# A scan kernel's last image: part of its norm beside its scans, one PSUM state less in half of the two-state steps, fp8 weights cast once

## The chip, the cores and the metric

The kernel runs on one core of a Trainium2 chip. The metric is device time in microseconds; three runs of the kernel before gave 11327.04, 11332.17 and 11333.0, median 11332.17. The profile is one further execution of 11308.41. Engines: PE (TensorE), DVE (VectorE), ACT (ScalarE), POOL (GpSimd), SP (SyncE, which issues the DMAs); PEld is PE's weight load.

## The reference, cut to what matters

Input is four images of 64 x 64 x 96. Layer 0 adds a selective-scan block with 192 channels to a group norm of x. Layer 1 does the same in the frequency domain: a 2-D real FFT, a block with 384 channels on 64 x 33 points, the inverse FFT. Layers 2 and 3 are token layers: linear attention, then a feed-forward net whose weights and activations are rounded to fp8 (e5m2). The block, shortened:

```python
xs = cross_scan(silu(conv(x_in)))          # 4 directions k: rows, columns, both reversed
dt, B, C = split(xs @ x_proj); delta = softplus(dt @ dt_w + dt_b)
h = h * exp(delta * A) + (delta * u) * B   # 16 states n per channel, serial in l
y = sum_n h * C (+ D * u)
y = layernorm(merge(y, 4 directions)) * silu(z)
out = y @ out_proj
q = lambda x: float_quantize(x, 5, 2)      # feed-forward: q(x), q(W), q(b)
```

## The kernel before, in words

**Scans.** Work is channels on partitions (three chunks c of 128), positions on the free axis, cut into segments of 512 (layer 0) or 512, 512, 384, 384, 320 (layer 1). There are six phases: two for layer 0 (two images each, 4 directions x 8 segments) and four for layer 1 (one image each, 4 x 5 segments). Directions run in the order 0, 2, 1, 3; 2 and 3 are reversed, 1 and 3 are those in which layer 1's rows lie in natural order. A segment has 12 steps: 4 quarters q of the states times 3 chunks c. A step has four states j, one DVE scan each (L710):

- ACT makes exp(delta A) (L682), in SBUF for j = 0, 1 and in PSUM for j = 2, 3. Inputs of j = 0, 1 are made by ACT (L646) and brought to PSUM by PE transposes (L678); those of j = 2, 3 by POOL (front_b, L700).
- State 0 of each step stays in PSUM and DVE multiplies it by C (multiply_kept, L728); in every other step state 3 too. The names in Step.kept, (0, 3) or (0,), say which. The other two or three states go to SBUF, and POOL multiplies them in one instruction (multiply, L747) after a small copy of the last column (L744); for kept states ACT copies that column (keep_state, L735).
- PE adds all products into acc by transposing matmuls (L757); close_chunk writes y to DRAM, one tile for directions 0 and 2, one for 1 and 3.

**Order.** Engines run in program order; scans() writes it out by hand. DMAs are all issued by SP, with eight in flight before one waits for an earlier one. All other work is a queue of tasks (Env), generators that yield between stages; each step has three slots, and rate / 3 says how many stages a slot gets. A stage that yields LATE runs in the slot at a step's end only. Each phase queues its tasks when its first segment begins: end1(b), the norm, out_proj, inverse FFT and tokens of image b, runs beside the scans of image b + 1. What is left when the scans end is run at once.

**Tail.** The last image's end1 runs after all scans, in a form with several workers (Env.wide > 1): gated (merge of directions L432, L438, mean L452, L456, variance L463, scaling L470, product with the gate L477 or L481) in three workers over the row blocks of 8, 8, 6, 6 and 5 rows, with out_proj (L1019) and the att write (L1028); then inverse (L1106, L1117) and tokens. tokens loads sixteen weight tiles per image (L1183) and casts w1, w2, b1, b2 of both layers to fp8 on DVE (L1189), b1 and b2 back to fp32 (L1191).

Of the kernel before, what the change touches and what calls it, by code (L numbers as in the profile page):

```python
# [7 lines left out]
F32 = mybir.dt.float32  # L8
F16 = mybir.dt.float16
F8 = mybir.dt.float8e5  # L10
# [8 lines left out]
NB, HH, WW, CH = 4, 64, 64, 96  # L19
# [4 lines left out]
SM = 512  # L24
LATE, BURST = "late", "burst"

RATES = [1.6, 2.35, 2.85, 2.85, 2.85, 2.85]
EXP_LN = "natural_log_exp_and_others"


# [127 lines left out]
class Block:  # L158
# [226 lines left out]
                    nc.sync.dma_start(out=gz[:, c, p0 * 64 : p1 * 64], in_=zh[:, : pr * 64])  # L385
                    yield

    def gated(self, E, g, io, out_proj):

# [6 lines left out]
        with E.pool(f"{cfg.pre}nm{g}") as sp:  # L396
            wo = sp.tile([P, C, self.w["wo"].shape[2]], F32, name=f"{cfg.pre}_wo_{g}", tag="wo")
            nc.sync.dma_start(out=wo, in_=self.w["wo"])

            def load(b, i, r, n):  # L400
# [10 lines left out]

            def worker(w):

                blocks = list(enumerate(cfg.rows))[w::W]
                todo = iter([(b, i, r + i, min(2, n - i)) for b, (r, n) in blocks for i in range(0, n, 2)])
                nxt = load(*next(todo))
                for _ in range(9 if W == 1 else 3):
                    yield
# [71 lines left out]
class Phase:  # L490

    def __init__(self, blk, g, io, needs, side, rate):
        self.blk, self.g, self.io, self.needs, self.side, self.rate = blk, g, io, needs, side, rate


class Seg:


    def __init__(self, ph, k, a, S, first, last):
        self.ph, self.blk, self.cfg = ph, ph.blk, ph.blk.cfg
        self.k, self.a, self.S, self.first, self.last = k, a, S, first, last
        self.rev = k >= 2
        self.nm = f"{self.cfg.pre}_{ph.g}_{k}_{a}"
        self.blocks = [(t, min(P, S - t)) for t in range(0, S, P)]
        full = S // P

        self.runs = [(0, full, P)] + ([(full, full + 1, S % P)] if S % P else [])
        self.bx, self.b, self.c, self.acc, self.u, self.after = {}, {}, {}, {}, None, None  # L510


class Step:


    def __init__(self, z, q, c):
        self.z, self.q, self.c = z, q, c
        self.nm = f"{z.nm}_{q}_{c}"
        self.kept = (0, 3) if (C * q + c) % 2 else (0,)
        self.hk = {}  # L520
        self.px, self.ay = {}, {}


def scans(tc, ctx, phases, ident):
# [14 lines left out]

    segs = []  # L540
    for ph in phases:
        for k in (0, 2, 1, 3):
            order = ph.blk.cfg.segs[::-1] if k >= 2 else ph.blk.cfg.segs
            segs += [Seg(ph, k, a, S, i == 0, i == len(order) - 1) for i, (a, S) in enumerate(order)]

    for z, after in zip(segs, segs[1:]):
        z.after = after
# [251 lines left out]
    with tc.manual_schedule(engines=IN_ORDER):  # L799
# [43 lines left out]
        for i, st in enumerate(steps):  # L843
            z, q, c, S = st.z, st.q, st.c, st.z.S
            nxt = steps[i + 1] if i + 1 < len(steps) else None
            if q == 0 and c == 0:
                after = z.after
                fresh = at == 0 or z.ph is not segs[at - 1].ph
                if fresh:
                    z.ph.io["y"] = [z.blk.dram_tile(f"y{j}", (2, z.cfg.L, C * P), z.ph.g) for j in range(2)]  # L850
                open_segment(z, segs[at - 1] if at else None)
                if after:
                    E.require(after.ph.needs[after.k % 2])
                pgen, pwants = prepare(after) if after else none, None
                at += 1
            if fresh and q == 0 and c == C - 1:
                for fn, arg in z.ph.side:
                    E.add((fn, arg), fn(E, arg))
            if c == 0:
                if q + 1 < NQ:  # L860
                    fetch_b(z, q + 1)
                elif after:
                    drain(pgen)
                    more = Pieces(after, 0, 4)
                    fetch_b(after, 0)
            if c == 1:
                if q + 1 < NQ:
                    fetch_c(z, q + 1)
                elif after:
                    fetch_c(after, 0)  # L870
            if older:
                add_rest(older)
            if before and 3 in before.kept:
                keep_state(before, 3)
                add_kept(before, 3)
            scan(st, 0)
            front_y(st, 2)
            if nxt:
                front_x(nxt)
            multiply_kept(st, 0)  # L880
            keep_state(st, 0)
            add_kept(st, 0)
            front_y(st, 3)
            long = burst()
            if before:
                multiply(before)
            if nxt:
                front_b(nxt)
            scan(st, 1)
            if nxt:  # L890
# [262 lines left out]
NT = LTOK // P  # L1153


def tokens(E, ins, consts, ident, x1, b, out):

# [5 lines left out]
    with E.pool(f"tk{b}") as sp:  # L1163
# [10 lines left out]
        def weights(ly):  # L1174

            nm, w, bufs = f"{b}_{ly}", {}, min(W, 2)
            for name, shape in (
                ("wqkv", [A, 3 * CH]), ("wqt", [CH, A]), ("wff", [CH, CH]), ("bff", [A, CH]),
                ("w1", [CH, 4 * CH]), ("w2", [P, 3, CH]), ("b1", [P, 3]), ("b2", [P, CH]),
            ):  # L1180
                t = w[name] = sp.tile(shape, F32, name=f"{name}_{nm}", tag=name, bufs=bufs)
                src = ins[f"l{ly}_{name}"]
                nc.sync.dma_start(out=t, in_=src.to_broadcast([P, CH]) if name == "b2" else src)  # L1183
            yield w
            for name in ("w1", "w2", "b1", "b2"):
                t = w[name]
                r = sp.tile(list(t.shape), F8, name=f"q{name}_{nm}", tag=f"q{name}", bufs=bufs)
                yield LATE
                nc.vector.tensor_copy(r, t, saturate=False)  # L1189
                if name in ("b1", "b2"):  # L1190
                    nc.vector.tensor_copy(t, r)  # L1191
                else:
                    w[name] = r

        loads = [weights(ly) for ly in (2, 3)]
        ws = [next(loads[0])] + ([next(loads[1])] if W > 1 else [])
# [3 lines left out]
        yield  # L1200
        yield
        for load in loads[: len(ws)]:
            yield from load

        def norm_all(nm):

# [155 lines left out]
        for ly in (2, 3):  # L1362
            nm = f"{b}_{ly}"
            if len(ws) < ly - 1:
                ws.append(next(loads[1]))
                yield from loads[1]
            q = ws[ly - 2]
            wq = q["wqkv"]
            if W == 1:
# [34 lines left out]
def build(tc, ins, consts, out):  # L1404
    nc = tc.nc
    with ExitStack() as ctx:
# [31 lines left out]
        x1 = [dram.tile([LTOK, CH], F32, name=f"x1_{b}", tag=f"x1_{b}") for b in range(NB)]  # L1438
        single = [dict() for _ in range(NB)]

        def flip0(E, g):
            yield from blk[0].flip(E, g, pairs[g])

# [11 lines left out]
        def begin1(E, b):  # L1455
# [2 lines left out]
            yield from blk[1].project(E, b, io)  # L1458
            yield from blk[1].gate(E, b, io)

        def end1(E, b):
            io = single[b]
            att = dram.tile([HH, WF, 2 * CH], F32, name=f"att_{b}", tag="att", bufs=NB)
            put = out1(att, b)
            yield from blk[1].gated(
                E, b, io, lambda E, *a: put(E, blk[1], *a)
            )
            yield
            rest = tokens(E, ins, consts, ident, x1[b], b, out)
# [15 lines left out]
        needs = [[None, (flip0, 0)], [(begin0, 1)] * 2]  # L1485
        with ExitStack() as inner:
            phases = [Phase(blk[0], g, pairs[g], needs[g], sides[g], RATES[g]) for g in range(2)] + [
                Phase(blk[1], b, single[b], [(begin1, b)] * 2, sides[2 + b], RATES[2 + b]) for b in range(NB)
            ]
            scans(tc, inner, phases, ident)  # L1490
        with ExitStack() as tail:
            alone(tail, end1, 3).finish()
# [113 lines left out]
```

## Time and profile before

| | us |
|---|---|
| median of the runs | 11332.17 |
| profiled execution | 11308.41 |
| its span, first to last instruction | 11306.6 |
| busy DVE / POOL / ACT / PE | 9899.2 / 9405.2 / 9384.7 / 9021.5 |
| layer 0, two phases | 217 to 2668, 2668 to 5112 |
| layer 1, four phases | 5112, 6582, 8007, 9476 to 10912 |
| tail: norm and out_proj / weights and inverse / tokens | to 11063 / to 11136 / to 11306.6 |

The mean granted clock of PE is 0.90. A line of groups reads: line, engine, operation, output <- inputs, shapes, count, busy time, mean ns of one, idle time of the engine before them and what ended it. In a table by stage each row is a window in us with the busy time (and count) of PE, PEld, DVE, ACT and POOL, the granted clock, the DMA engines' busy share, and GB/s. In the chain of waits each piece is start, length, and what ran or was waited for.

### The profile page before, as it was taken

To read this page: it belongs to the slowest core of one execution; us is meant where nothing else is said; L and a number is where in the kernel's file an instruction comes from. 1 tells how busy PE (TensorE), PEld (TensorE's weight loads), DVE (VectorE), ACT (ScalarE), POOL (GpSimd) and SP (SyncE) were. 2 spreads that over 40 slices of the span, in tenths; PEclk is the share of its full clock that TensorE was granted. 3 is DMA by queue.
4 is the path that set the end of the run, shared out by engine and by line. 5 is a ranking of instruction groups with operands and counts; after the bars stand their busy time and mean duration, and the time that the engine had idled before them with its cause. 6 is when DMAs were issued, how large, how long until landed. Compare 5 with 4: busy or idle time off the path is not lost. (4 is left out here: it accounts for less than half of the span.)

```text
span 11306.6 us, 163986 instructions
## 1 busy us (share of the span) xinstructions
PE 9021.5 (80%) x54944; PEld 6600.5 (58%) x54944; DVE 9899.2 (88%) x10695; ACT 9384.7 (83%) x19648; POOL 9405.2 (83%) x7464
## 2 busy tenths in 40 slices
PE   5678788777888888888899888887788777887775
PEld 2555555556666656656676665665566555665554
DVE  6889999889999998999888798989989889889864
ACT  3779999999888998998778788878888788878853
POOL 2999999989988998998788798878888779888750
PEclk9889999889999999999889899998899888998887
DMA  5655555556666556555543545442244223542242
GB/s 146 144 130 130 133 129 123 155 156 153 156 161 140 129 144 140 134 142 169 156 134 119 136 136 157 150 113 94 92 145 138 93 90 107 158 120 94 82 130 38
DMA packets 1208406, 1468.97 MB, mean 130 GB/s; under 512 B 482759, under 2 KB 1020559, under 8 KB 1149063
## 3 DMA queue, kind: packets, MB, share of 16 engines
q1 hardware_dynamic: 1207559, 1458.48, 47.8%
q8 instruction: 434, 7.11, 0.3%
q14 instruction: 413, 3.38, 0.1%
HBM read 1221.74 MB, written 236.50 MB: 129 GB/s over the span
## 5 line engine op out<-in xcount | busy, mean ns | idle before, releaser
L747 POOL TENSOR_TENSOR h_l<-h_l,bc_l 128x1536 f32<-128x1536 f32 (+2 forms) x1728 | 4567.8, 2643 | 184.0 <-DVE h_l L710 68.1
L700 POOL TENSOR_TENSOR h_l<-du_l,bc_l 128x512 f32<-128x512 f32 (+2 forms) x3456 | 3966.7, 1170 | 770.1 <-PE acc_l L757 718.1
L646 ACT ACTIVATE bx_l<-dut_l,bt_l 128x192 f32<-128x192 f32 (+2 forms) x6272 | 2756.4, 499 | 0.3
L757 PEld LDWEIGHTS acc_l<-ident,h_l 128*128 128x128 f32 (+1 forms) x15840 | 2047.7, 155 | 689.2 <-issue 325.9
L757 PE MATMUL acc_l<-ident,h_l 128*128 128x128 f32 (+1 forms) x15840 | 2326.3, 299 | 135.9 <-POOL h_l L747 135.6
L682 ACT ACTIVATE ax_l<-delta_l,l_alog 128x512 f32<-128x512 f32 (+2 forms) x3456 | 2140.4, 667 | 0.0
L710 DVE TENSOR_TENSOR_SCAN h_l<-b_l,state_l,h_l 128x512 f32<-128x512 f32 (+2 forms) x1263 | 1389.1, 1121 | 114.2 <-ACT b_l L682 106.6
L678 PE MATMUL b_l<-ident,bx_l 128*128 128x128 f32 (+1 forms) x6817 | 1200.5, 295 | 227.1 <-DVE h_l L710 220.2
L678 PEld LDWEIGHTS b_l<-ident,bx_l 128*128 128x128 f32 (+1 forms) x6817 | 842.9, 149 | 829.5 <-DVE h_l L710 476.8
L682 ACT ACTIVATE b_l<-delta_l,l_alog 128x512 f32<-128x512 f32 (+2 forms) x1948 | 1221.0, 627 | 107.7 <-DVE k_l L728 32.0
L710 DVE TENSOR_TENSOR_SCAN b_l<-ax_l,state_l,b_l 128x512 f32<-128x512 f32 (+2 forms) x842 | 956.5, 1136 | 194.1 <-PE b_l L678 191.3
L757 PE MATMUL acc_l<-ident,k_l 128*128 128x128 f32 (+1 forms) x5117 | 836.9, 294 | 334.3 <-DVE k_l L728 320.1
L678 PE MATMUL ab_l<-ident,bx_l 128*128 128x128 f32 x5312 | 900.9, 298 | 246.5 <-DVE h_l L710 237.7
L682 ACT ACTIVATE ab_l<-delta_l,l_alog 128x512 f32<-128x512 f32 x1326 | 913.8, 689 | 149.0 <-DVE h_l L710 70.0
L678 PEld LDWEIGHTS ab_l<-ident,bx_l 128*128 128x128 f32 x5312 | 648.5, 151 | 622.2 <-DVE h_l L710 452.4
L710 DVE TENSOR_TENSOR_SCAN h_l<-ax_l,state_l,b_l 128x512 f32<-128x512 f32 (+2 forms) x841 | 951.2, 1131 | 42.1 <-PE b_l L678 40.4
L710 DVE TENSOR_TENSOR_SCAN h_l<-ab_l,state_l,h_l 128x512 f32<-128x512 f32 x743 | 920.2, 1261 | 73.2 <-ACT ab_l L682 46.7
L728 DVE TENSOR_TENSOR k_l<-b_l,bc_l 128x512 f32<-128x512 f32 (+2 forms) x1460 | 895.4, 613 | 50.2
L757 PE MATMUL acc_l<-ident,hk_l 128*128 128x128 f32 x3976 | 641.3, 296 | 328.3 <-DVE hk_l L728 315.5
L757 PEld LDWEIGHTS acc_l<-ident,k_l 128*128 128x128 f32 (+1 forms) x5117 | 627.3, 150 | 437.2 <-DVE k_l L728 368.7
L297 PE MATMUL pc_l<-pad_l,l_dg 128*128 128x512 f32 (+2 forms) x1656 | 783.9, 561 | 57.2 <-ACT uh_l L275 42.9
L757 PEld LDWEIGHTS acc_l<-ident,hk_l 128*128 128x128 f32 x3976 | 494.1, 152 | 409.7 <-DVE hk_l L728 337.3
(252 smaller groups left out, 15015.4 us busy)
## 6 DMA issues: line engine op xcount, KB each, us to landing
bc_l<-l_xd_l SPq DMA_DIRECT2D x640, 512.0 KB
bc_l<-l_xd_l SPq DMA_DIRECT2D x512, 256.0 KB
bc_l<-l_xd_l SPq DMA_DIRECT2D x128, 1024.0 KB
bc_l<-l_xd_l SPq DMA_DIRECT2D x128, 768.0 KB
us_l<-l_u SPq DMA_DIRECT2D x96, 768.0 KB
l_y<-y_l SPq DMA_DIRECT2D x288, 256.0 KB
yt_l<-l_y SPq DMA_DIRECT2D x264, 192.0 KB
yt_l<-l_y SPq DMA_DIRECT2D x128, 384.0 KB
```

Of the source, the lines that this page charges most:

```text
L297: nc.tensor.matmul(pc[:, : n * 64].rearrange("p (r w) -> p r w", w=64), diag[:, t, :], pad[:, r - p0 + dy : r - p0 + dy + n, dx : dx + 64] ...
L646: nc.scalar.activation(t[:n, b, :, ch], z.dut[:n, b, :, ch], AF.Copy, scale=z.bt[:n, b, m : m + 1])
L678: nc.tensor.transpose(pb[:, t : t + n], st.z.bx[st.q, j][:n, b, st.c], ident[:n, :n])
L682: nc.scalar.activation(out, z.delta[:, st.c, : z.S], AF.Exp, scale=z.blk.A[:, st.c, z.k, n : n + 1])
L700: nc.gpsimd.tensor_tensor(st.h[:, 1 + j, :S], st.z.du[:, st.c, :S], st.z.b[st.q][:, j, :S], ALU.mult)
L710: nc.vector.tensor_tensor_scan(h[:, ::step], a[:, ::step], b[:, ::step], 0.0 if z.first else z.state[st.c][:, n : n + 1], ALU.mult, ALU.add,)
L728: nc.vector.tensor_tensor(hk[:, : z.S], kept_at(st, j), z.c[st.q][:, j, : z.S], ALU.mult)
L747: nc.gpsimd.tensor_tensor(h, h, z.c[st.q][:, 1 : 1 + m, : z.S], ALU.mult)
L757: nc.tensor.matmul(z.acc[st.c][:m, b, :], hc[:, t : t + m], ident, start=(first and b == 0), stop=(last and b == 0), is_transpose=True,)
```

## The change

1. The last image's phase runs its directions in the order 0, 2, 3, 1, so that the last direction goes forward in natural row order and finishes row blocks one by one (the segments 512, 512, 384, 384, 320 are the blocks of 8, 8, 6, 6, 5 rows). When segments 1, 2, 3 of that direction have begun, norm and out_proj of blocks 0, 1, 2 are queued as side tasks; the tail does blocks 3 and 4 only.
2. Layer 1's steps keep two states in PSUM in one of four steps instead of one of two. Layer 0 is as before.
3. The fp8 weights are loaded and cast once, as a task of the first phase, into the constant pool. tokens loads four weight tiles a layer, not eight, and casts none.
4. Rates of side work rise from 2.85 to 2.95, and to 3.1 in the last phase.

```diff
-RATES = [1.6, 2.35, 2.85, 2.85, 2.85, 2.85]
+RATES = [1.6, 2.35, 2.95, 2.95, 2.95, 3.1]
...
-    def gated(self, E, g, io, out_proj):
+    def gated(self, E, g, io, out_proj, part=slice(None)):
...
-                blocks = list(enumerate(cfg.rows))[w::W]
+                blocks = list(enumerate(cfg.rows))[part][w::W]
...
-        self.kept = (0, 3) if (C * q + c) % 2 else (0,)
+        self.kept = (0, 3) if (C * q + c) % (2 * z.cfg.KI) == 1 else (0,)
...
-        for k in (0, 2, 1, 3):
+        for k in ph.order:
...
+            if ph.parts and k == ph.order[-1]:
+                for i, z in enumerate(segs[1 - len(order) : -1]):
+                    z.task = (ph.parts, i)
...
+            if z.task and q == 0 and c == C - 1:
+                fn, arg = z.task
+                E.add(z.task, fn(E, arg))
...
+def quantized(E, cp, ins, quant):
+    nc = E.nc
+    shapes = (("w1", [CH, 4 * CH]), ("w2", [P, 3, CH]), ("b1", [P, 3]), ("b2", [P, CH]))
+    with E.pool("qw") as sp:
+        loaded = []
+        for ly in (2, 3):
+            for name, shape in shapes:
+                t = sp.tile(shape, F32, name=f"{name}_{ly}", tag=f"{name}{ly}")
+                src = ins[f"l{ly}_{name}"]
+                nc.sync.dma_start(out=t, in_=src.to_broadcast([P, CH]) if name == "b2" else src)
+                loaded.append((ly, name, shape, t))
+        for _ in range(6):
+            yield
+        for ly, name, shape, t in loaded:
+            keep = cp if name in ("w1", "w2") else sp
+            r = keep.tile(shape, F8, name=f"q{name}_{ly}", tag=f"q{name}{ly}")
+            yield LATE
+            nc.vector.tensor_copy(r, t, saturate=False)
+            if keep is sp:
+                r, q = cp.tile(shape, F32, name=f"k{name}_{ly}", tag=f"k{name}{ly}"), r
+                nc.vector.tensor_copy(r, q)
+            quant[ly][name] = r
...
-                ("w1", [CH, 4 * CH]), ("w2", [P, 3, CH]), ("b1", [P, 3]), ("b2", [P, CH]),
...
-            for name in ("w1", "w2", "b1", "b2"):
-                t = w[name]
-                r = sp.tile(list(t.shape), F8, name=f"q{name}_{nm}", tag=f"q{name}", bufs=bufs)
-                yield LATE
-                nc.vector.tensor_copy(r, t, saturate=False)
...
+            w.update(quant[ly])
+            return w
...
+        for _ in range(6 if W == 1 else 2):
+            yield
...
+        def last1(E, i):
+            yield from norm1(E, NB - 1, slice(i, i + 1))
...
+            yield from norm1(E, b, slice(len(CFG1.rows) - 2 if b == NB - 1 else 0, None))
...
-            [(flip0, 0), (begin0, 1), (gate0, 0), (gate0, 1)],
+            [(flip0, 0), (begin0, 1), (gate0, 0), (gate0, 1), (quant0, 0)],
...
+            phases.append(
+                Phase(blk[1], b, single[b], [(begin1, b)] * 2, sides[2 + b], RATES[2 + b], (0, 2, 3, 1), last1)
+            )
```

norm1 calls gated for the row blocks it is given, with the out_proj of before.

More of the change, by code (lines that the diff above doesn't have):

```diff
@@ L395, in gated @@
         u, gz = io["u"][cfg.nat], io["gz"]
-        with E.pool(f"{cfg.pre}nm{g}") as sp:
-            wo = sp.tile([P, C, self.w["wo"].shape[2]], F32, name=f"{cfg.pre}_wo_{g}", tag="wo")
+        first = list(enumerate(cfg.rows))[part][0][0]
+        with E.pool(f"{cfg.pre}nm{g}_{first}") as sp:
+            wo = sp.tile([P, C, self.w["wo"].shape[2]], F32, name=f"{cfg.pre}_wo_{g}_{first}", tag="wo")
             nc.sync.dma_start(out=wo, in_=self.w["wo"])
@@ L412, in worker @@
             def worker(w):
-                blocks = list(enumerate(cfg.rows))[w::W]
+                blocks = list(enumerate(cfg.rows))[part][w::W]
                 todo = iter([(b, i, r + i, min(2, n - i)) for b, (r, n) in blocks for i in range(0, n, 2)])
+                if not blocks:
+                    return
                 nxt = load(*next(todo))
@@ L490, with __init__ @@
 class Phase:
-    def __init__(self, blk, g, io, needs, side, rate):
+    def __init__(self, blk, g, io, needs, side, rate, order=(0, 2, 1, 3), parts=None):
         self.blk, self.g, self.io, self.needs, self.side, self.rate = blk, g, io, needs, side, rate
+        self.order, self.parts = order, parts
 class Seg:
@@ L509, in __init__ @@
         self.runs = [(0, full, P)] + ([(full, full + 1, S % P)] if S % P else [])
-        self.bx, self.b, self.c, self.acc, self.u, self.after = {}, {}, {}, {}, None, None
+        self.bx, self.b, self.c, self.acc, self.u, self.after, self.task = {}, {}, {}, {}, None, None, None
 class Step:
@@ L1153, with tokens @@
 NT = LTOK // P
-def tokens(E, ins, consts, ident, x1, b, out):
+def quantized(E, cp, ins, quant):
[21 more added lines that the diff above has]
+    yield
+def tokens(E, ins, consts, ident, x1, b, out, quant):
     nc = E.nc
@@ L1178, in weights @@
                 ("wqkv", [A, 3 * CH]), ("wqt", [CH, A]), ("wff", [CH, CH]), ("bff", [A, CH]),
-                ("w1", [CH, 4 * CH]), ("w2", [P, 3, CH]), ("b1", [P, 3]), ("b2", [P, CH]),
             ):
                 t = w[name] = sp.tile(shape, F32, name=f"{name}_{nm}", tag=name, bufs=bufs)
-                src = ins[f"l{ly}_{name}"]
-                nc.sync.dma_start(out=t, in_=src.to_broadcast([P, CH]) if name == "b2" else src)
-            yield w
-            for name in ("w1", "w2", "b1", "b2"):
-                t = w[name]
-                r = sp.tile(list(t.shape), F8, name=f"q{name}_{nm}", tag=f"q{name}", bufs=bufs)
-                yield LATE
[L1189 to L1196, printed above, removed]
+                nc.sync.dma_start(out=t, in_=ins[f"l{ly}_{name}"])
+            w.update(quant[ly])
+            return w
+        ws = [weights(ly) for ly in ((2, 3) if W > 1 else (2,))]
         yield
@@ L1199, in tokens @@
         nc.sync.dma_start(out=x, in_=x1.rearrange("(p t) c -> p t c", t=NT))
[L1200 to L1203, printed above, removed]
+        for _ in range(6 if W == 1 else 2):
+            yield
         def norm_all(nm):
@@ L1364, in tokens @@
             if len(ws) < ly - 1:
-                ws.append(next(loads[1]))
-                yield from loads[1]
+                ws.append(weights(3))
             q = ws[ly - 2]
@@ L1439, in build, with quant0 @@
         single = [dict() for _ in range(NB)]
+        quant = {2: {}, 3: {}}
+        def quant0(E, g):
+            yield from quantized(E, cp, ins, quant)
         def flip0(E, g):
@@ L1459, in begin1, with norm1 @@
             yield from blk[1].gate(E, b, io)
-        def end1(E, b):
[L1462 to L1469, printed above, removed]
+        atts = [dram.tile([HH, WF, 2 * CH], F32, name=f"att_{b}", tag=f"att{b}") for b in range(NB)]
+        def norm1(E, b, part):
+            put = out1(atts[b], b)
+            yield from blk[1].gated(E, b, single[b], lambda E, *a: put(E, blk[1], *a), part)
+            yield
+        def last1(E, i):
+            yield from norm1(E, NB - 1, slice(i, i + 1))
+        def end1(E, b):
+            att = atts[b]
+            yield from norm1(E, b, slice(len(CFG1.rows) - 2 if b == NB - 1 else 0, None))
+            rest = tokens(E, ins, consts, ident, x1[b], b, out, quant)
             if E.wide > 1:
@@ L1487, in build @@
             phases = [Phase(blk[0], g, pairs[g], needs[g], sides[g], RATES[g]) for g in range(2)] + [
-                Phase(blk[1], b, single[b], [(begin1, b)] * 2, sides[2 + b], RATES[2 + b]) for b in range(NB)
+                Phase(blk[1], b, single[b], [(begin1, b)] * 2, sides[2 + b], RATES[2 + b]) for b in range(NB - 1)
             ]
+            b = NB - 1
+            phases.append(
+                Phase(blk[1], b, single[b], [(begin1, b)] * 2, sides[2 + b], RATES[2 + b], (0, 2, 3, 1), last1)
+            )
             scans(tc, inner, phases, ident)
```

## The prediction

> **What bounds the kernel now.** First the page: busy tenths in 40 slices. The scans fill slices 1 to 38, and in them no engine stands out; the last slice and a half is a tail in which POOL does nothing and the others idle.
>
> ```profile
> PE   5678788777888888888899888887788777887775
> DVE  6889999889999998999888798989989889889864
> ACT  3779999999888998998778788878888788878853
> POOL 2999999989988998998788798878888779888750
> ```
>
> Then busy time by stage. The four phases of block 1 (one image each) are 5112 to 10912; then the tail: norm and out_proj to 11063, weights and inverse to 11136, tokens to the end. Columns: window, length, busy time of PE, PE weight load, DVE, ACT, POOL, then clock, DMA share, GB/s.
>
> ```profile
> 5112.00:6582.00 1470.00, 1289.69 (x7829) 952.53 (x7828) 1233.57 (x1410) 1152.68 (x2285) 1189.87 (x1013) 0.89 0.49 141
> 6582.00:8007.00 1425.00, 1174.25 (x7151) 842.10 (x7149) 1273.77 (x1467) 1198.05 (x2439) 1207.70 (x1026) 0.91 0.41 126
> 8007.00:9476.00 1469.00, 1161.77 (x7218) 857.55 (x7219) 1322.87 (x1552) 1233.10 (x2565) 1213.62 (x1016) 0.88 0.37 111
> 9476.00:10912.00 1436.00, 1133.90 (x7114) 832.02 (x7113) 1312.84 (x1531) 1200.14 (x2489) 1209.19 (x1013) 0.89 0.37 112
> 10912.00:11063.00 151.00, 108.56 (x588) 86.13 (x588) 25.52 (x47) 28.50 (x51) 1.44 (x3) 0.86 0.58 142
> ```
>
> DVE leads in phases 2 to 4 (1323 of 1469), POOL is 60 to 110 us behind it. Two segments of 512 show the two limits: without DVE side work both are full (first line: DVE 69.5 and POOL 69.6 of 70.7), with some DVE is full and POOL has 5 us left.
>
> ```profile
> 5928.40:5999.10 70.70, 64.61 (x387) 45.03 (x386) 69.48 (x67) 58.39 (x113) 69.56 (x52) 1.00 0.33 108
> 7347.60:7422.10 74.50, 61.14 (x395) 46.97 (x393) 73.39 (x77) 62.08 (x121) 69.53 (x53) 0.93 0.39 115
> ```
>
> Last the chain of waits in the tail: loads first, then the last pair of rows, then SP's weight loads.
>
> ```profile
> 10939.69 11.58 DMA zb_l<-l_gz
> 11028.29 0.91 PE py_l L432 x6
> 11049.77 12.61 PE po L1019 x66
> 11066.40 4.33 SPq L1183
> 11074.90 4.95 SPq L1183
> 11089.98 6.22 DMA at<-att
> ```
>
> **1. Tail: three of five norm blocks leave it.** Before, scans end at 10911.6, the last y write is issued at 10918.1, the first py matmul runs at 10927.2. Blocks 0 to 2 go first in the three workers; blocks 3 and 4 share the second round: their last pair of rows lands at 11028.3 and from there to the att write (11062.9) are 34.6 us. After, only that second round is left. It still has to load 4 pairs of up to 960 KB, two z tiles (1056 KB), wo and the half pair: about 6.6 MB. The slices here moved 230 to 300 GB/s, so at 250 that is 26 us from about 10921: the last pair lands near 10948 in place of 11028, -80. Bounds: -65 if the two-deep yt buffers make the last pair wait for PE, -95 if it runs at 300 GB/s with less queueing. In the built order 5 of the last moved block's 43 stages come after the final scan, and its att write sits in SP's queue between the tail's first two loads: two po groups and copies, about +3 (0 to 6).
>
> **2. Tail: eight of sixteen weight loads leave SP.** From 11064.1 to 11081.5 SP issues them, held twice (4.3 and 5.0 us in the chain). The first hold is for the landing of the att write eight DMAs earlier, about 9 us after its issue; in the built order that wait stays with eight loads too, and the inverse needs the landing anyway. So of the 17.4 us about 8 go (0 to 12). The casts of the tail (1.4 us a layer, DVE idle around them) hide behind this and count nothing. Tail together: -85.
>
> **3. fp8 once.** Images 0 to 2 lose two layers each of six casts (L1189, L1191). In the scans these are dear:
>
> ```profile
> 7539.66 2.59 DVE L1191 CAST b<-qb 128x96 f32<-128x96 fp8e5 x1
> 8806.13 0.36 DVE L1189 CAST qw<-w 96x384 fp8e5<-96x384 f32 x1 [6.95 <-DMA w<-in_l_w]
> ```
>
> The same b2 cast takes 0.21 in the tail, where POOL rests. Over the six layers the casts sum to 27.7, and DVE stood 3.5, 7.0 and 0.6 us for the weights' DMA: 38.7. Scans stand directly before and after most of them, but some of these segments have other idle time; I take 0.7 of it, -27 (-38 to -10, where the wait passes to the tok load, which is used 15 us after its issue). The one pass in phase 0 costs two layers: 2.8 at the tail's price, 9.2 at that of the phases (27.7/6 = 4.6 a layer). It runs in 2596.9 to 2668.2, where DVE has 1.8 of 71.3 idle and POOL 3.1. The Trainium skill (SBUF — State Buffer, "Who interferes with whom") says that a cast in a two-port mode and a GpSimd instruction exclude each other for the whole instruction; that speaks for the high end, since POOL is full there: +8. Its sixteen loads land during six stages (two scan steps, some 12 us); if not, the scans queued on DVE behind the first cast wait, up to 7.
>
> **4. The moved norm beside scans.** A block of 512 has on DVE 3 subtractions of 0.675, 3 scalings of 0.738 and 3 products of 0.671 = 6.25; one of 384, 5.07. Three blocks: 17.6. ACT and PE get their parts too, but DVE is fullest there: +17 (+10 to +28, if PE, in order, holds transposes behind a late yt load; the stages give each load 9 stages, three steps, and the same code beside earlier images shows no yt or ut load among the 60 largest waits). In SP's queue the block's loads stand before broadcasts of B and C fetched a quarter ahead. Rates of 2.95 and 3.1 move side work earlier and add none: 0 (-8 to +8).
>
> **5. One of four steps with two states in PSUM.** In block 1, 3 of 12 steps in a segment go from two DVE products to one. DVE loses 0.691, 0.557 or 0.491 (S 512, 384, 320) each: 36 a phase (8 x 3 x 0.691 + 8 x 3 x 0.557 + 4 x 3 x 0.491). POOL's product grows from 2.366 to 3.453, 1.818 to 2.634, 1.544 to 2.222: 54 a phase. POOL goes to about 1244 to 1267, DVE to 1198 to 1287: balanced. ACT loses 240 copies of 0.147. I put the 80 segments by idle time: in 24 DVE idles at most 5 us and POOL has room: the whole saving, -46; in 22 it idles 5 to 8: half, -19; in 28 more than 8 (PE, DMA or ACT holds): nothing; in 6 POOL has less idle than it gets: +10. Of the 24 some have only 5 us on POOL and keep 2, so coupling takes back some 15: -40. Bounds: -131 if every product taken away (all but the 6) was on the path; +60 if a quarter or so of POOL's 215 is. The three-state form waits longer as well: POOL's 3-column state copy idles 274.5 us in 696 for DVE's last scan, the 2-column one 24.2. The skill speaks against this step (GPSIMD Engine Reference, "Engine selection": an elementwise product of two inputs belongs on VectorE, GpSimd being about half as fast). By it the step is a loss, 1.09 us bought for 0.69, +54 a phase. The rows agree on the price, but DVE's product reads one operand in PSUM and stays at 690 to 694 ns whatever POOL does, and the engine relieved is the fuller: I follow the segments.
>
> **Sum.** -85 - 27 + 8 + 17 - 40 = -127. The profiled execution is 11308.4 (span 11306.6 and 1.8 around it) and goes to 11181; the median of the runs is 23.8 higher, so 11205.
>
> **Rivals.**
> - DVE relief in full: -131 in place of -40. For it: L728 and L710 run back to back in many segments; against it: PE and ACT carry most of the chain. 11114. Chance 0.20.
> - The tail is bound by its chain, not by its loads: it gives 45, the casts 10. For it: 34.6 us of the round are PE, ACT and DVE in turn. 11205 + 40 + 17 = 11262. Chance 0.20.
> - POOL becomes the bound of block 1's scans: its 215 us on the path, nothing from DVE. Place: front_b and the product of each step, which DVE's third scan waits for. It ends slower once the step costs over 87 instead of giving 40, that is from 40% of the 215; in full 11205 + 40 + 215 = 11460. Against it: POOL idles 980 us in the four phases. Chance 0.04.
> - It doesn't do what it says: the moved norm finds no idle engine and the gains go in it and in the casts of phase 0; about 11330. Against it: the built order ends the side work with the scans. Chance 0.05.
>
> The forecast has 0.51, its own range 11165 to 11245. 0.2% (22.7 us) is about what this measurement can tell from no change. Faster 0.91, same 0.05, slower 0.04. The range takes in most of the first two rivals: 11110 to 11280.
>
> **What would show it.** Tail from the last scan to the end about 310 instead of 395, last py pair some 30 us after the last y write; no CAST of weights after 2668; L728 1152 + 1200 times instead of 1152 + 1440; block 1's phases together 50 us shorter, POOL at most 88% in them. Wrong: POOL over 92% with DVE waiting for L700, or a tail over 340.

## The result and the profile after

The median went from 11329.6 to 11285.99 us (six runs each). The ratio is 0.9958, 95% interval 0.9946 to 0.9971: about 48 us, where 127 had been forecast. The profiled execution took 11266.7 (span 11264.9) in place of 11308.4. Line numbers of the changed kernel are 3 to 10 higher than those of before up to the inverse, and more in tokens, where L1217 is the load of weights: L754 and L707 are POOL's product and front_b, L717 the scan, L764 the adding matmul, L735 multiply_kept. One profile is one execution: a first phase whose code is that of before took 2450 to 2465 us in ten of the profiles of this text, so a difference of ten or so between two of them can be chance.

First the slices, DVE and POOL of the changed kernel. POOL, at 5 in the last slice but one before, is at 7 there now: the stretch without scans is shorter.

```profile
DVE  6889999889999998999878697988988989878974
...
POOL 2999999988898998998789798988988889878970
```

Then the stages of the changed kernel in the columns of before (window, length, busy PE, PEld, DVE, ACT, POOL, clock, DMA share, GB/s): the four phases of block 1, then what is left of norm and out_proj.

```profile
5136.00:6602.00 1466.00, 1276.00 (x7858) 943.02 (x7855) 1200.51 (x1350) 1149.09 (x2240) 1238.69 (x1011) 0.90 0.49 141
6602.00:8031.00 1429.00, 1190.62 (x7201) 855.43 (x7202) 1248.70 (x1418) 1209.05 (x2445) 1263.08 (x1029) 0.90 0.42 126
8031.00:9478.00 1447.00, 1151.55 (x7217) 850.63 (x7215) 1278.52 (x1471) 1216.97 (x2487) 1268.89 (x1021) 0.89 0.38 115
9478.00:10955.00 1477.00, 1174.05 (x7375) 867.67 (x7375) 1278.80 (x1472) 1197.47 (x2450) 1256.47 (x1007) 0.89 0.40 117
10955.00:11019.00 64.00, 41.40 (x213) 32.42 (x212) 8.69 (x18) 10.10 (x21) 1.89 (x1) 0.79 0.45 116
```

The tail from the last scan to the end went from 395.0 to 310.3: -84.7, and the norm's share of it from 151 to 64. DVE's busy time in the four phases fell by 33, 25, 44 and 34, POOL's rose by 49, 55, 55 and 47, both as forecast. But the phases as a whole are not 50 us shorter: they measure 1465, 1430, 1447 and 1476 where they were 1470, 1426, 1469 and 1435, 19 more in the sum. The last one alone is 41 longer. The first phase of layer 0, which now holds the casts, takes 2473.7 where it took 2451.0. So the tail paid in full, and the scans, layer 0's included, gave back half of it.

The chain of waits in the tail, changed kernel. The last pair of rows (yt, ut) has landed at 10987.7, 33 us after the last scan. Eight loads of weights stand on SP's queue ahead of the inverse, where sixteen stood; one of them has a hold of 4.2 us. The second hold of before has passed to the inverse's own first load (L1108), which takes 3.6 where it took 0.4.

```profile
10987.70 1.65 PE py_l L435 x6
...
11029.16 4.22 SPq L1217
...
11036.21 3.63 SPq L1108
...
11048.67 6.40 DMA at<-att
```

Last, casts of the fp8 weights in the first phase, from the timeline (start, length). The first and the third are the same form on the same engine, 0.17 us and 3.44. The two lines of POOL below them tell why: each long cast lies beside a product of POOL (L754) and ends within 0.1 us of it. The short one began in a gap of POOL.

```profile
2644.87 0.17 DVE L1187 CAST kb<-qb 128x3 f32<-128x3 fp8e5 x1
...
2650.63 3.44 DVE L1187 CAST kb<-qb 128x96 f32<-128x96 fp8e5 x1
...
2667.22 3.44 DVE L1187 CAST kb<-qb 128x3 f32<-128x3 fp8e5 x1
...
2650.57 3.43 POOL L754 TENSOR_TENSOR h_l<-h_l,bc_l 128x1536 f32<-128x1536 f32 x1 [1.90 <-DVE h_l L717]
...
2667.21 3.43 POOL L754 TENSOR_TENSOR h_l<-h_l,bc_l 128x1536 f32<-128x1536 f32 x1 [2.84 <-DVE qb L1184]
```

### The profile page after: what moved, and what is told of

Its sections match the earlier page's. It is cut to its first block, busy times and chain, and to the rows that moved or that the text cites. A ratio compares the mean times of both kernels' runs of the same rounds, so it can differ in the third digit from the quotient of the medians.

```text
span 11264.9 us, 163660 instructions
## 1 busy us (share of the span) xinstructions
PE 9018.3 (80%) x54944; PEld 6606.2 (59%) x54944; DVE 9757.3 (87%) x10419; ACT 9356.3 (83%) x19465; POOL 9611.9 (85%) x7464
## 4 chain that ended last, share of the span: by engine, by line
PE 25%; ACT 25%; POOL 22%; DVE 16%; issue 7%; DMA 3%; SPq 1%; POOLq 0%; DVEq 0%; ACTq 0%
POOL h_l L754 10%; POOL h_l L707 9%; PE acc_l L764 7%; DVE h_l L717 7%; ACT bx_l L653 5%; ACT ax_l L689 5%; ACT b_l L689 3%; DVE b_l L717 3%; PE b_l L685 2%; DVE ab_l L717 2%; PE pc_l L297 2%; PE pi_l L210 1%; PE pp_l L578 1%; POOL du_l L611 1%; ACT ab_l L689 1%
## 5 line engine op out<-in xcount | busy, mean ns | idle before, releaser
L754 POOL TENSOR_TENSOR h_l<-h_l,bc_l 128x1536 f32<-128x1536 f32 (+2 forms) x1728 | 4781.0, 2767 | 205.0 <-DVE h_l L717 84.2
L707 POOL TENSOR_TENSOR h_l<-du_l,bc_l 128x512 f32<-128x512 f32 (+2 forms) x3456 | 3964.7, 1169 | 659.2 <-PE acc_l L764 603.4
L653 ACT ACTIVATE bx_l<-dut_l,bt_l 128x192 f32<-128x192 f32 (+1 forms) x6272 | 2756.7, 499 | 0.3
L764 PEld LDWEIGHTS acc_l<-ident,h_l 128*128 128x128 f32 x16656 | 2125.9, 154 | 839.6 <-POOL h_l L754 388.5
L764 PE MATMUL acc_l<-ident,h_l 128*128 128x128 f32 x16656 | 2422.8, 298 | 242.5 <-POOL h_l L754 241.1
L717 DVE TENSOR_TENSOR_SCAN h_l<-b_l,state_l,h_l 128x512 f32<-128x512 f32 (+2 forms) x1376 | 1496.1, 1110 | 129.5 <-ACT b_l L689 113.6
L717 DVE TENSOR_TENSOR_SCAN b_l<-ax_l,state_l,b_l 128x512 f32<-128x512 f32 (+2 forms) x846 | 960.3, 1135 | 257.0 <-PE b_l L685 255.5
L717 DVE TENSOR_TENSOR_SCAN h_l<-ab_l,state_l,h_l 128x512 f32<-128x512 f32 x803 | 992.6, 1262 | 77.6 <-ACT ab_l L689 42.9
L764 PE MATMUL acc_l<-ident,k_l 128*128 128x128 f32 (+1 forms) x4733 | 790.4, 296 | 323.6 <-DVE k_l L735 317.0
L717 DVE TENSOR_TENSOR_SCAN h_l<-ax_l,state_l,b_l 128x512 f32<-128x512 f32 (+2 forms) x846 | 956.2, 1130 | 66.4 <-PE b_l L685 63.1
L735 DVE TENSOR_TENSOR k_l<-b_l,bc_l 128x512 f32<-128x512 f32 (+2 forms) x1335 | 827.2, 620 | 45.9
L764 PEld LDWEIGHTS acc_l<-ident,k_l 128*128 128x128 f32 (+1 forms) x4733 | 585.8, 151 | 420.9 <-DVE k_l L735 361.7
L764 PE MATMUL acc_l<-ident,hk_l 128*128 128x128 f32 x3628 | 588.0, 295 | 258.7 <-DVE hk_l L735 246.1
L717 DVE TENSOR_TENSOR_SCAN ab_l<-ax_l,state_l,ab_l 128x512 f32<-128x512 f32 x496 | 632.1, 1274 | 124.3 <-PE ab_l L685 123.6
```

Source lines behind the costliest of these rows:

```text
L653: nc.scalar.activation(t[:n, b, :, ch], z.dut[:n, b, :, ch], AF.Copy, scale=z.bt[:n, b, m : m + 1])
L707: nc.gpsimd.tensor_tensor(st.h[:, 1 + j, :S], st.z.du[:, st.c, :S], st.z.b[st.q][:, j, :S], ALU.mult)
L717: nc.vector.tensor_tensor_scan(h[:, ::step], a[:, ::step], b[:, ::step], 0.0 if z.first else z.state[st.c][:, n : n + 1], ALU.mult, ALU.add,)
L735: nc.vector.tensor_tensor(hk[:, : z.S], kept_at(st, j), z.c[st.q][:, j, : z.S], ALU.mult)
L754: nc.gpsimd.tensor_tensor(h, h, z.c[st.q][:, 1 : 1 + m, : z.S], ALU.mult)
L764: nc.tensor.matmul(z.acc[st.c][:m, b, :], hc[:, t : t + m], ident, start=(first and b == 0), stop=(last and b == 0), is_transpose=True,)
```

## Experiments: each part alone

The first reading of this profile was a theory called T here. In the changed kernel PE waits for POOL's product, which in block 1 it hardly did before. T says that this wait holds PE's transposes, so that the DVE time that the fourth edit frees turns into idle time of DVE, and that edit gives nothing. Its rivals: the edit is a loss (A); the denser side work is the loss (B); the moved norm is dearer than 17 us (C). Each part was put alone on the kernel before, except that the moved norm came with the rates. A difference in us is the ratio's, on some 11320 us, and so is the interval; the medians beside it can be up to 9 us off that.

**Two states in PSUM in one of four steps, alone.**

```diff
-        self.kept = (0, 3) if (C * q + c) % 2 else (0,)
+        self.kept = (0, 3) if (C * q + c) % (2 * z.cfg.KI) == 1 else (0,)
```

> The kernel before with one of four steps with two states in PSUM, nothing else. Theory T (POOL's longer product comes later, PE, in order, waits for it, and the DVE time saved turns into waiting for PE's transposes): DVE busy in block 1 about 140 us less, idle as much more, time within 10 us of before. Rival A (the step is itself a loss, POOL's 215 us partly on the path): +20 to +50. Rival B (the step is worth what was predicted, the loss lies in the denser side work): -40.

Measured: 11284.35 against 11318.33, ratio 0.9963 (0.9949 to 0.9978): -42 (-58 to -25), as B had it. A falls, and T falls as far as it said that the edit gives nothing. In part T is right: in the profile DVE is 129 us less busy in block 1's four phases (5014 for 5143) and they are only 9 shorter (5791 for 5800), so most of the freed time became idle time, as the prediction had it too. The wait that had suggested T is there all the same. PE's largest waits in block 1 of this kernel, and below them two of before (line, what was waited for, us in total, times, longest):

```profile
PE acc_l L757 <- DVE k_l L728: 144.5, 109, 5.8
PE acc_l L757 <- POOL h_l L747: 121.6, 110, 4.4
PE acc_l L757 <- DVE hk_l L728: 114.2, 91, 7.5
...
PE acc_l L757 <- DVE k_l L728: 166.1, 130, 6.2
PE acc_l L757 <- DVE hk_l L728: 164.4, 131, 7.2
```

POOL's was not among the eleven largest before. What PE waits for has changed its name, and the kernel is 42 us faster with it: a new wait in a list is no cost until the time says so.

**The new rates alone.**

```diff
-RATES = [1.6, 2.35, 2.85, 2.85, 2.85, 2.85]
+RATES = [1.6, 2.35, 2.95, 2.95, 2.95, 3.1]
```

> The kernel before with the rates 2.95, 2.95, 2.95, 3.1, nothing else. Theory T: -5 to +10, some segments lose what others win. Rival B (denser side work, the inverse FFT above all, falls into short segments that it overfills): +20 to +40, most of it in the last phase, in its third direction as run second. The prediction said 0 (-8 to +8).

Measured: 11376.43, ratio 1.0046 (1.0033 to 1.0059): +52, more than any of the ranges. This is the largest single loss, and it does no work at all. The four directions of the last phase, in the order in which they run, first of before:

```profile
9476.00:9820.00 344.00, 286.34 (x1794) 212.20 (x1794) 318.29 (x373) 291.49 (x589) 300.20 (x253) 0.93 0.50 147
9820.00:10192.00 372.00, 317.32 (x2110) 230.15 (x2109) 327.83 (x381) 298.27 (x619) 298.75 (x248) 0.93 0.46 125
10192.00:10556.00 364.00, 269.96 (x1654) 198.48 (x1653) 340.63 (x399) 315.15 (x675) 306.26 (x260) 0.86 0.27 88
10556.00:10912.00 356.00, 260.28 (x1563) 191.18 (x1562) 326.07 (x381) 295.23 (x609) 303.98 (x255) 0.86 0.27 91
```

and with the rates alone:

```profile
9510.00:9862.00 352.00, 301.82 (x1886) 223.07 (x1885) 318.22 (x376) 287.21 (x585) 294.94 (x245) 0.94 0.51 151
9862.00:10272.00 410.00, 321.02 (x2054) 230.32 (x2053) 338.49 (x393) 317.02 (x669) 302.86 (x253) 0.87 0.36 103
10272.00:10651.00 379.00, 278.48 (x1693) 207.43 (x1692) 343.46 (x404) 318.88 (x680) 307.13 (x260) 0.85 0.26 85
10651.00:10973.00 322.00, 236.07 (x1400) 171.92 (x1399) 301.52 (x345) 263.10 (x530) 297.50 (x249) 0.89 0.30 100
```

Side work has left the fourth direction (DVE 25 less, ACT 32 less), which is 34 shorter. The second got only 11 of DVE and 19 of ACT and is 38 longer, with DVE idle for 71.5 of 410 where it was 44 of 372. The first three together are 61 longer for 13 us more of DVE, so the loss lies where the work is denser; the emptied direction gives back more than the DVE time that left it. The profile of the kernel with 3.1 in the last phase alone (below) repeats the pattern: +20, +22, +14 and -25 for the four directions. The last phase is not all of it: block 1's four phases differ by +12, +29, -5 and +28, and what the second one lost was not followed up.

The waits of the second direction's first segments tell what holds: with the rates (9862 to 9997)

```profile
POOL h_l L700 <- PE acc_l L757: 44.3, 16, 4.3
DVE b_l L710 <- PE b_l L678: 21.8, 9, 5.9
```

and before (9820 to 9946)

```profile
POOL h_l L700 <- PE acc_l L757: 19.5, 15, 2.4
DVE b_l L710 <- PE b_l L678: 9.2, 10, 1.5
```

The engines that do the scan wait for PE, in as many waits as before that last twice as long. In this stretch image 2's inverse FFT (L1117, L1133) now stands in PE's order, in segments of 320 and 384; before it ran from 9953 on, in those of 384 and 512. That this place of the FFT is the cause was not tested. PE's clock is not what doubles these waits: in the two stretches it is 0.94 and 0.95. In the rest of the direction it is 0.83 where it was 0.92, and how much of the 38 us that makes stays open; over the whole kernel the runs were granted 0.896 with the rates and 0.898 before.

**The moved norm, with the new order of directions and the rates.** The diff is items 1 and 4 of the change.

> The kernel before with the new order of directions, norm and out_proj of three blocks of the last image as side tasks, and the new rates; PSUM states and fp8 casts as before. All theories: tail from the last scan to the end about 395 to 318. T: scans +17 for the moved norm and 0 to +10 for the rates, so -50 to -60. Rival B: scans +40 to +60, so -20 to -40. Rival C (the moved norm costs far more than 17): the last direction of the last phase is over 40 us longer than the one that ran last before.

Measured: 11323.45, ratio 1.0004 (0.9996 to 1.0012). If the costs add up, it gives 47 once the rates' 52 are taken off. Against the profile with the rates alone, the last phase is 30.1 longer (1493.4 for 1463.3), 23.5 of it in the direction that runs last, and the tail 74.4 shorter (314.4 for 388.8). T's -50 to -60 and B's -20 to -40 both miss. C does not hold: the direction that runs last takes 345.2, where the last one took 355.4 before and 321.7 with the rates alone, not 40 more. B is right that the rates lose, and had them too cheap.

**The fp8 weights once, alone.** The diff is item 3 of the change.

> The kernel before with the fp8 weights loaded and cast once, in the first phase. Phase 0 about +14 (twelve casts of 14.6 us in the profile of the changed kernel), tail -8. T: images 0 to 2 give 15 to 25, so -10 to -20 in all. If the waits only pass on to the token load: -5 to +5. The prediction: -27 + 8 - 8 = -27.

Measured: 11307.85, ratio 0.999 (0.9982 to 0.9998): -11 (-20 to -2), inside T's range, which lets the images give 15 to 25. In the profile the first phase is 13.3 longer, the tail 9.8 shorter; the four phases of block 1 differ by -2.6, +2.3, -2.9 and +1.2. Only part of the tail's 9.8 belongs to the loads: from the att write to the first matmul of the inverse it is 21.6 us for 25.8, so 4. The rest lies in the norm, which the edit leaves alone (tails without the edit and with the norm in place measure 388 to 395). And so the 38.7 us of casts and waits that the images lose gave 2 us in this pair of profiles. The runs allow more: -11 less some +14 for the first phase and -4 for the loads leaves about -21, an estimate from these numbers.

The parts add up: -42 + 5 - 11 = -48, what the whole change measured. A coupling of up to some 20 us could hide in the intervals, but none is needed; the question is what the rates cost.

## Experiments: why a rate costs 52 us

Theory D: a denser row of side stages costs more than the free stretch at the end gives back. Theory L: a changed rate changes which stage meets which step, and that is luck.

```diff
-RATES = [1.6, 2.35, 2.85, 2.85, 2.85, 2.85]
+RATES = [1.6, 2.35, 2.9, 2.9, 2.9, 2.9]
```

> The kernel before with rate 2.9 in the four phases of layer 1. The rates alone (2.95, 3.1) cost 0.46%, about 52 us. Theory D (a denser row of side stages costs more per stage than it frees at the end of a phase): a smooth cost, +15 to +25 here. Theory L (at a rate near 3 the stages stay in the same place of the step, and which stage meets which step is luck): no smooth line, -20 to +60.

Measured: 11367.14, ratio 1.0033 (1.002 to 1.0045): +37.

```diff
+RATES = [1.6, 2.35, 2.8, 2.8, 2.8, 2.8]
```

> The kernel before with rate 2.8 in the four phases of layer 1; some 18 token stages of image 2 are left to run after the last scan, perhaps +5 to +10. D: scans -15 to -25, so -5 to -20 in all. L: -20 to +60.

Measured: 11338.29, ratio 1.0013 (1.0004 to 1.0021): +15.

```diff
+RATES = [1.6, 2.35, 2.85, 2.85, 2.85, 3.1]
```

> The kernel before with rate 3.1 in the last phase only. D and the profile of both new rates (last phase +28, second of layer 1 +29): +25 to +30. If the loss sits in the 2.95 of the other phases: 0 to +8. If it is all in the last phase: +50.

Measured: 11362.76, ratio 1.0028 (1.0017 to 1.0038): +32. More than half of the loss is the last phase's. But no smooth line goes through 2.8, 2.85, 2.9 and 2.95 (+15, 0, +37, +52), and D's ranges for 2.8 and 2.9 both missed; D alone does not explain it.

**The changed kernel with 2.85 in three phases.**

```diff
-RATES = [1.6, 2.35, 2.95, 2.95, 2.95, 3.1]
+RATES = [1.6, 2.35, 2.85, 2.85, 2.85, 3.1]
```

> The changed kernel with 2.85 in the first three phases of layer 1, 3.1 in the last. In the built order last1 of block 2 and the last stage of block 1 (some 43 stages) then run after the last scan, which costs 10 to 25. D: three phases give 24 to 30, so -20 to +0 against the changed kernel, that is 0.9940 to 0.9960 of before. L: the other edits have moved the stages anyway, anything from -30 to +40.

Measured: 11257.19, ratio 0.9928 (0.9916 to 0.9941), some 34 faster than the changed kernel's 0.9958, although the stages left over make the tail 20 longer (330.4 from the last scan to the end). D's range missed on the good side, and L's just.

**Pairs.** A stage marked LATE waits for the slot at a step's end; meanwhile the rate runs up, and that slot takes two stages. In the order of the program 121 slots of block 1 do so before, and somewhat under 40 more with the rates alone. Theory M says that the second of a pair waits in its engine's order for the first, some 0.9 us each. The dose was raised:

```diff
-            slot(None, hold=long)
+            slot(None, hold=long, skip=st.nm.startswith("l1"))
...
+            if skip:
+                return
             for _ in range(min(int(due), 1 + (due >= 2.0))):
```

> The kernel before, layer 1, with the second slot of each step left empty: what it would have taken runs as a pair in the slot at the step's end. Same rate, same stages in the same steps or one later, nothing left over. Slots that take two stages: 805 of block 1's 2880 in place of 121. Theory M (a pair of stages in one slot costs about 0.9 us, since the second stage waits in its engine's queue for the first one's result, and the scans behind it wait too; from a fit of the step times of seven profiles): +300 to +650. Theory L (placement is luck, pairs as such cost nothing): -40 to +60.

Measured: 11483.35, ratio 1.0145 (1.0131 to 1.0159): +164 for 684 more pairs, 0.24 us each. The edit also empties each step's second slot, so the 0.24 holds for both together. By it the pairs that the rates add are worth some 9 of the 52. M names a cost of the right sign and has its size wrong by a factor of four.

**No LATE.** Then the other end, with hardly a pair left:

```diff
-        if self.wants not in (None, kind):
+        if self.wants is BURST and kind is not BURST:
             return False
```

> The kernel before with stages marked LATE allowed in every slot, so that no backlog builds up: pairs beside block 1's scans 8 in place of 121, stages beside scans the same, none left over. M: -60 to -110. L: -40 to +40. If the mark LATE is worth more than the pairs it causes (its DVE and POOL work then stands ahead of scans): +20 to +100.

Measured: 11266.15, ratio 0.9954 (0.9942 to 0.9967): -52, between M's range and L's. At 0.24 us, 113 pairs explain 27 of it. A rival for the rest is the clock: these runs were granted 0.901 to 0.903, those of before beside them 0.893 to 0.899. Among the runs of before, a clock higher by 0.001 goes with a time 3 to 4.5 us shorter, so 0.006 may stand for some 18 to 27 us (an estimate from these runs). Whether the clock makes the kernel shorter or the fuller kernel gets the higher clock, no run here tells. This kernel is also denser than before in the second and third phases, by some 16 stages each in the order of the program, and these two take 2879 us in place of 2895. So a denser phase is not always a longer one.

**Places alone, and rates without a backlog.** Two kernels keep the rate and only shift image 0 to 2's end1, by one empty stage each, or four:

```diff
+            for _ in range(1 if E.wide == 1 else 0):
+                yield
             io = single[b]
```

> The kernel before with one empty stage ahead of each end1 of the images 0 to 2: the same work at the same rate, each stage one slot later. Theory D (density) and the backlog theory: within 8 us of before. Theory L (which stage meets which step decides, and before stands at a good place): +10 to +50; a gain of over 10 would also be L.

Measured: 11320.33, ratio 1.0006 (0.9996 to 1.0016): +7, not told apart from no change.

> The kernel before with four empty stages ahead of each end1 of the images 0 to 2 (each stage four slots, later eight and twelve slots after its old place; nothing left over). D and backlog: within 8 us of before. L: +10 to +50, or a gain of over 10.

Measured: 11305.31, ratio 0.9986 (0.9977 to 0.9994): -16, a gain of over 10, as only L had it. An edit that adds no work moves the time by up to 16 us, so places count, and before does not stand at the best of them; but two shifts that give +7 and -16 do not make +52 likely as luck.

> The kernel before with LATE stages allowed in every slot and the new rates. Without the rates it is 0.9954 of before. Backlog theory: the rates cost nothing where no backlog arises, 0.9945 to 0.9965. D: the rates cost their 40 to 60 here too, 0.9990 to 1.0010. L: anything between.

Measured: 11301.25, ratio 0.9988 (0.9979 to 0.9997): the rates cost 38 on top of the kernel without LATE. The backlog theory falls, and D's range is just missed.

So of the 52 about 38 (some 21 to 55, by the two intervals) stay when the backlog is gone, and pairs make some 9. In the profiles of the pair without LATE the rates cost 18 in the last phase (directions +5, +9, +14 and -10) and 29 in the first phase of block 1. The uneven filling, in which directions that get more stages lose more than the emptied one gives back, is what the rows show for the last phase. For the other phases it is argued, not shown. Why 2.8 and 2.9 do not lie on a line with it stays open; shifts of place of the size seen, about 16, would cover 2.8 and hardly 2.9.

## Experiments: a faster version

**Casts ahead of the scans.** The sixteen loads are issued in the stretch before the first scan and cast there, with the rates of 2.85 and 3.1.

```diff
-            [(flip0, 0), (begin0, 1), (gate0, 0), (gate0, 1), (quant0, 0)],
+            [(flip0, 0), (begin0, 1), (gate0, 0), (gate0, 1)],
...
+        fp8 = quantized(begin, cp, head.enter_context(begin.pool("qw")), ins, quant)
...
+        begin.add(None, fp8)
+        next(fp8)
```

> The changed kernel with rates 2.85, 2.85, 2.85, 3.1 and the fp8 casts in the stretch before the scans, where POOL rests. Against the same without that move (0.9928 of before): the twelve casts of 14.6 us beside full POOL become some 3, so -8 to -14, ratio 0.9915 to 0.9922; first phase 2452 to 2460 in place of 2471. If the sixteen loads delay the first stretch: up to 5 less gain.

Measured: 11248.57, ratio 0.9939 (0.9927 to 0.9952). The time doesn't tell it from 0.9928, so the gain is not shown in the end time. In the profile the casts behave as expected, in all 2.5 us where they were 14.6, and the first phase takes 2454.5 in place of 2471.1; the first scan starts at 218.2 in place of 216.5. The groups of DVE ahead of the scans (count, busy, mean ns, idle before):

```profile
L1181 DVE CAST qw<-w 96x384 fp8e5<-96x384 f32 (+1 forms) x4 | 1.2, 320 | 0.0
L1184 DVE CAST kb<-qb 128x3 f32<-128x3 fp8e5 (+1 forms) x4 | 0.7, 186 | 0.1
L1181 DVE CAST qb<-b 128x3 fp8e5<-128x3 f32 (+1 forms) x4 | 0.6, 179 | 1.7 <-DMA b<-in_l_b 1.7
```

**The same without LATE.** The edit is that of the kernel without LATE above.

> The same as the kernel with the casts ahead of the scans, with stages marked LATE allowed in every slot: pairs beside block 1's scans about 30 in place of 140, and block 2 of the moved norm ends with the scans. M: -60 to -120 against it, ratio near 0.983. L: -40 to +40. If the mark is worth more than the pairs: +20 to +100.

Measured: 11177.07, ratio 0.9878 (0.9862 to 0.9895): 138 faster than before and some 70 faster than the last, inside M's range. It beats both kernels. That it comes within 30 us of the forecast's 11205 is chance, since it has an edit that the forecast did not know. Of the 70 the tail makes 21 (309.1 for 330.1), as no stages are left over at the end; M's 0.24 for some 110 fewer pairs would make 26. Its runs were granted 0.901 to 0.906, the last kernel's 0.897 to 0.901, so the clock is a rival here too. Its four phases and the tail:

```profile
5105.00:6562.00 1457.00, 1275.72 (x7835) 946.11 (x7833) 1201.41 (x1350) 1146.15 (x2237) 1238.54 (x1011) 0.90 0.48 142
6562.00:8001.00 1439.00, 1182.38 (x7205) 852.80 (x7204) 1244.05 (x1414) 1204.51 (x2436) 1262.46 (x1027) 0.91 0.41 125
8001.00:9410.00 1409.00, 1140.21 (x7243) 837.36 (x7243) 1275.63 (x1476) 1222.02 (x2499) 1269.25 (x1022) 0.90 0.38 115
9410.00:10859.00 1449.00, 1154.44 (x7398) 853.72 (x7397) 1276.81 (x1472) 1195.91 (x2449) 1256.90 (x1007) 0.91 0.41 121
10859.00:11168.00 309.00, 175.08 (x1270) 133.68 (x1268) 119.81 (x222) 112.48 (x299) 5.03 (x5) 0.70 0.26 54
```

DVE and POOL have the busy times of the changed kernel to within 5 us in every phase, and its tail is as long; the four phases take 64 us less in the sum (5754 for 5818). The difference there is idle time of both engines.

## Why the prediction was right or wrong

- **Tail, norm blocks: right.** -80 (-65 to -95) was worked out from the loads of the second round; the moved norm makes the tail 74.4 shorter. The last pair landed 33 us after the last scan; "some 30 us" after the last y write had been forecast. (The "4 pairs" of its working should be five; its 6.6 MB are the sum with five.) The chain shows po groups of the moved block until 10965 ahead of it. The rival in which the tail gives only 45 falls.
- **Eight weight loads: right in kind, half in size.** -8 (0 to -12) was forecast; 4 came. The prediction kept the first hold of SP's queue and let the second go with the loads; it passed to the inverse's first load, 3.6 us.
- **fp8 once: the sign right, the size wrong.** With the loads, -27 was forecast and -11 measured. The one pass was put at 8; the twelve casts took 14.6 in the profile. The first phase takes 2470 on average in three profiles with the pass and 2456 in ten without, so about 14. Here the Trainium skill (SBUF — State Buffer, "Who interferes with whom") had pointed to the right side, and this trace agrees: a cast that meets POOL's product lasts as long as the product, 3.44 us beside 3.43, and 0.2 alone. "I take 0.7 of it, -27" for images 0 to 2 gave 2 us in the profile and some 21 by the runs, an estimate. What took the rest is not settled: taking the casts out also shifts every later stage, and such a shift alone was worth -16 to +7.
- **Moved norm: mechanism right, size off.** The term of 17 counted DVE's instructions only; the last phase took 30.1 for it, just over the forecast's upper bound of 28. In the last direction DVE is 13 us busier and the time 23.5 longer. PE got 41 us more there and ACT 15; that these make the difference was not tested.
- **Rates: wrong, and this is the step that failed.** "Rates of 2.95 and 3.1 move side work earlier and add none: 0 (-8 to +8)." They cost 52 (37 to 67). The prediction priced side work by the instructions that it issues, and took its place for free. In the last phase, three directions got 13 us more of DVE's work and became 61 longer, while the fourth lost 25 and gave back 34. By which wait each of the 61 came is shown for one stretch only (the scans' engines waiting for PE).
- **Two states in PSUM: right.** -40 forecast from idle times segment by segment, -42 (-58 to -25) measured. From the skill's rule (GPSIMD Engine Reference, "Engine selection") the prediction had worked out a loss of 54 a phase; the measurement goes against that here. POOL's busy time in the four phases rose by 208 (5029 for 4820) and they did not become longer, so its new time fell into its idle time. The rival in which DVE's relief counts in full (-131) and that in which POOL becomes the bound both fall.

In sum: -74 (norm out of the tail) + 30 (norm beside scans) + 52 (rates) - 42 (PSUM) - 11 (fp8 with its loads) = -45, within 3 of the measured -48. The forecast's -127 misses that by 82: 52 for the rates, 16 for fp8, 13 for the norm beside scans and small terms. With the rates at 0 the same sum gives -97, inside the forecast's own range; no run has the whole change at the old rates.

## What to carry to other kernels

Price a change of *when* work is done like a change of work: in this kernel, whose engines run in a written order, the same stages at another rate cost 0.5%, more than any single edit of its arithmetic gave. Before changing a rate or a priority together with other edits, measure it alone, and look at each stretch for what it lost and what it got back, not at busy totals: DVE's was 9901 us with the rates and 9899 before. A new wait in the list (PE on POOL, 122 us) is no verdict: the kernel that has it was the faster one.

## What was not expected of the hardware

- A small DVE cast that meets a product of POOL ends with it: 3.44 us beside a product of 3.43, where the same 128x3 conversion from fp8 takes 0.17 in a gap of POOL; 14.6 us for twelve that take 2.5 where POOL rests.
- With one slot of each step emptied into the next, 684 more pairs of stages cost 0.24 us each.
- A shift of unchanged work by four slots was worth 0.14% (0.06 to 0.23).
